# Layer 3's features dealt out through DRAM instead of transposed on TensorE, in a four-layer graph attention kernel

## The chip, the cores and the metric

One core of a Trainium2 chip runs the whole kernel. The metric is the time of one execution on the device in microseconds (us). The engines are TensorE (PE in the profile, its weight loads PEld), VectorE (DVE), ScalarE (ACT), GpSimd (POOL) and SyncE (SP), which here only issues transfers.

## The reference

There are 128 independent graphs of 128 nodes with 512 features, and an adjacency matrix for each. Four layers of graph attention follow each other, each as `x = x + layer(relu(layernorm(x)), adj)`:

```
h  = maximum(layernorm(x), 0)
# layer 0: scores from h @ (W.T a1), h @ (W.T a2); leaky relu, mask, softmax; elu(attn @ h)
# layer 1: xl = h @ W1 (4 heads x 256); attention by head, bias, elu; then a second
#          one-head layer: (elu(..) @ W2), attention over the nodes, bias
# layer 2: scores from h @ w_src, h @ w_dst; softmax; attn @ h
# layer 3: xp = h @ W_proj, split into 8 heads of 64 features
#   scores[h,i,j] = leaky_relu(a_src[h,i] + a_dst[h,j] + b[h]), masked by adj
#   out = relu(softmax(scores) @ xp), heads side by side
```

All is in float32. Layers 1 and 3 project h with a matrix of weights, so TensorE needs h with the features on the partitions; h is made with the nodes on the partitions.

## The kernel before

A graph is one stream of steps, written as a Python generator (`graph`). It runs `layer0` to `layer3` on a tile `xt` of 128 nodes x 512 features, held on chip until the result is written. Up to 13 graphs are in flight (`FLYING`), so that one graph's matmuls fill another's waits. No loop order is written by hand: a planner (`Scheduler`) goes through all streams with a cost for every step and issues, one after the other, the step that can start first. Among steps of the same engine that can start about as early, the older graph goes first, with a due time for each step from a rehearsed graph. The result is one fixed order of instructions on each engine, and each engine works its own list in order. Each wait for data is a semaphore wait in that order.

SyncE's queue carries nearly all transfers. The planner lets 8 of them be under way (`LANES`).

The last five graphs are late (`LATE`): they take other ways, with fewer trips through DRAM, since there is no other graph left to fill the waits.

Steps that matter here:

- `norm_relu` gets mean and variance on VectorE, the factor on GpSimd, and writes h with one ScalarE instruction.
- `transposed` turns up to four 128 x 128 blocks on TensorE into one PSUM bank, and ScalarE copies the bank into a tile. Layers 1 and 3 call it on the four blocks of h, giving `ht`.
- `projected` multiplies `ht`, four blocks as the weights on the array, with `w1x` (three column parts of 344) or `wpx` (two parts of 264). In float32 each block takes two passes: two weight loads and two matmul instructions.
- `rows_in_dram` puts the scores of each head, a column per head, into rows: VectorE transposes 32 x 32 squares, four transfers write the rows to DRAM, and one transfer reads them back to all 128 partitions as `e`.
- `exchanged` moves attention's blocks through DRAM after or before VectorE's 32 x 32 transposes, so TensorE does not transpose them.

A VectorE transpose works on squares of 32 x 32 (`Q` = 32, `R` = 4 squares across the partitions). Its result is a whole transpose only when the squares also trade places, which is what a trip through DRAM can do.

Nearly all instructions are issued from the planner's one line 302, so the profile tells them apart by tile names and shapes: `bank` is a PSUM bank, `ident` the identity that TensorE's transposes use, `h`, `ht`, `wpx`, `w1x` as above, `x` layer 3's projected features (and the second half of layer 1's), `e` the scores, `et` their transposed form, `r` the transposed score columns, `d` the rows in DRAM.

Of the kernel before, what the change touches and what calls it, by code (L numbers as in the profile page):

```python
# [9 lines left out]
F32 = mybir.dt.float32  # L10
I32 = mybir.dt.int32
AF = mybir.ActivationFunctionType
# [314 lines left out]
def kernel(  # L327
# [24 lines left out]
    B, P, D = x.shape  # L352
# [43 lines left out]

    E1, E2, E3 = 2 * H1, 2, 2

    def rows_of(name, n, *shape):
# [19 lines left out]

    def few(to, values):
        with nc.allow_non_contiguous_dma(reason="at most 1024 values, once"):
            nc.scalar.dma_start(out=to, in_=values)

    def setup():
        for i, a in enumerate((l0_a1, l0_a2)):
            few(a0[:, :, i], a.rearrange("(c p) o -> p (c o)", p=P))  # L430
        for i, a in enumerate((l1_src1, l1_dst1)):
            few(a1[:, :, i], a.rearrange("h (c p) -> p (h c)", p=P))
        few(b1, l1_b1.rearrange("(c p) -> p c", p=P))

        w0 = []
        for c in range(KC):
            if c % 2 == 0:
                pair = yield tile_of("e3", 3, H3 * P)
                pair = pair.rearrange("p (c f) -> p c f", c=2)
            w0.append(pair[:, c % 2])  # L440
            yield S.dma_start(out=w0[c], in_=l0_w[c * P : (c + 1) * P])
        yield Fork(fold_u(w0))
        yield from load(0)
        for c in range(KC):
            yield S.dma_start(out=w1x[c][:, E1:], in_=l1_w1[c * P : (c + 1) * P])
        yield Fork(fold_w1())
        yield Fork(load_turned(0))
        yield from load(1)
        yield from load(2)
        vecs = []  # L450
        for row in (l1_src2, l1_dst2):
            vecs.append((yield tile_of("x2", 2, E2 + D))[:, :D])
            yield S.dma_start(out=vecs[-1], in_=row[0].partition_broadcast(P))
        for c in range(FC):
            yield S.dma_start(out=w2x[c][:, E2:], in_=l1_w2[c * P : (c + 1) * P])
        yield Fork(fold_w2(vecs), 3)
        yield S.dma_start(out=b2[:, E2:], in_=l1_b2.partition_broadcast(P))
        yield from load(3)
        yield from load(4)
        for t, row in (w_src, l2_src), (w_dst, l2_dst), (b_l2, l2_b), (b_l3[:, 0], l3_batt):  # L460
            yield S.dma_start(out=t, in_=row.partition_broadcast(P))
        yield from load(5)
        for c in range(KC):
            yield S.dma_start(
                out=wpx[c][:, :, E3:],
                in_=l3_wp[c * P : (c + 1) * P].rearrange("p (h k) -> p h k", h=H3),
            )
        wa = yield tile_of("e3", 3, H3 * P)
        wa = wa[:, : H3 * 2 * K3]
        yield S.dma_start(out=wa, in_=l3_watt.rearrange("h k -> (h k)").partition_broadcast(P))  # L470
        yield Fork(fold_w3(wa), 6)
        for b in range(6, min(FLYING + AHEAD, B)):
            yield from load(b)
# [68 lines left out]
        sched.reached.add("wp")  # L542


    def norm_relu(xt):

        n = nc.vector.BN_STATS_DIM
        st = yield tile_of("st", 6, n + 5)
        yield V.bn_stats(st[:, :n], xt)
        mean, var = st[:, n : n + 1], st[:, n + 1 : n + 2]  # L550
        yield V.bn_aggr(st[:, n : n + 2], st[:, :n])
        ve, rstd, nmr = (st[:, i : i + 1] for i in range(n + 2, n + 5))
        yield G.tensor_scalar(ve, var, EPS, None, ALU.add)
        yield G.tensor_tensor(out=rstd, in0=ve, in1=minus_half, op=ALU.pow)
        yield G.tensor_scalar(nmr, mean, rstd, -1.0, ALU.mult, ALU.mult)
        h = yield tile_of("h", 4, D)
        yield A.activation(out=h, in_=xt, func=AF.Relu, bias=nmr, scale=rstd)
        give_back(st)
        return h

# [44 lines left out]
        yield S.dma_start(out=to, in_=d.rearrange("m b r f -> (m b) (r f)"))  # L605
        return to

    def rows_in_dram(cols, n, heads_inside=False):

        r = yield tile_of("r", 5, Q)  # L610
        yield V.transpose(r, cols)
        d = dram.tile([R, n, Q] if heads_inside else [n, R, Q], F32, tag=f"d{n}", name="d")
        yield Group(
            [
                S.dma_start(
                    out=d[c] if heads_inside else d[:, c], in_=r[c * Q : c * Q + n]
                )
                for c in range(R)
            ]
        )  # L620
        give_back(r)
        return d.rearrange("n c b -> (n c b)").partition_broadcast(P)
# [150 lines left out]

    def layer1(xt, mask, late):
        h = yield from norm_relu(xt)
        ht = yield from transposed(blocks_of(h), "ht", 3)
        give_back(h)
        yield Until("w1")
        fx = yield tile_of("xl", 3, E1 + HF)

        e = yield tile_of("e1", 3, H1 * P)
        if late:
            heads = e.rearrange("p (h c b) -> p h c b", h=H1, b=Q)
        else:
            heads = e.rearrange("p (c h b) -> p h c b", h=H1, b=Q)
        heads = [heads[:, j] for j in range(H1)]

        def rows():
            d = yield from rows_in_dram(fx[:, :Q], H1, not late)
            yield S.dma_start(out=e, in_=d)  # L790

        fork = yield from projected(ht, KC, w1x, 3, columns(fx, 3), rows)
        give_back(ht[0])
        xl = fx[:, E1:]
        yield Join(fork)
        mask = mask.rearrange("p (c b) -> p c b", b=Q)
        c, rz = yield from attention(fx[:, H1:E1], heads, heads, mask)
        for j in range(H1):
            yield A.activation(out=heads[j], in_=heads[j], func=AF.Copy, scale=rz[:, j : j + 1])
        give_back(c)  # L800
        if late:
            et = yield from transposed(blocks_of(e), "et1", 2)
        else:

            yield V.transpose(e, e)
            to = yield from exchanged(e, "et1", 2)
            et = to.rearrange("p (r h b) -> p h r b", h=H1, b=Q)
            et = [et[:, j] for j in range(H1)]
        give_back(e)
        y = yield tile_of("y1", 2, FC, P)  # L810
        for g in range(0, FC, 4):
            po = yield bank()
            yield Group(
                [
                    T.matmul(
                        po[:, (c - g) * P : (c - g + 1) * P],
                        lhsT=xl[:, c * P : (c + 1) * P],
                        rhs=et[c * P // F1],
                        start=True,
                        stop=True,  # L820
                    )
                    for c in range(g, g + 4)
                ]
            )
            yg = y[:, g : g + 4, :]
            yield V.tensor_tensor(
                yg,
                po.rearrange("p (j q) -> p j q", q=P),
                b1[:, g : g + 4].unsqueeze(2).to_broadcast([P, 4, P]),
                ALU.add,  # L830
            )
            give_back(po)

            yg = yg.rearrange("p c q -> p (c q)")
            t = yield tile_of("t", 5, 4 * P)
            yield V.tensor_scalar(t, yg, 0.0, None, ALU.min)
            yield A.activation(out=t, in_=t, func=AF.Exp)
            yield V.scalar_tensor_tensor(yg, t, -1.0, yg, ALU.add, ALU.max)
            give_back(t)
        give_back(fx, et[0])  # L840
        yield Until("w2")
        gx = yield tile_of("x2", 2, E2 + D)

        yl = [y[:, c] for c in range(FC)]
        yield from projected(yl, FC, w2x, 2, columns(gx, 2), plus=columns(b2, 2))
        give_back(y)
        pa, c, rz = yield from attended(gx[:, 1:2], gx[:, 0:1], mask, gx[:, E2:], late)
        give_back(gx)
        yield V.scalar_tensor_tensor(xt, pa, rz, xt, ALU.mult, ALU.add)
        give_back(pa, c)  # L850
# [10 lines left out]
        yield V.scalar_tensor_tensor(xt, pa, rz, xt, ALU.mult, ALU.add)  # L861
        give_back(pa, c)

    def layer3(xt, mask, late):

        h = yield from norm_relu(xt)
        ht = yield from transposed(blocks_of(h), "ht", 3)
        give_back(h)
        yield Until("wp")

        fx = yield tile_of("x3", 3, H3, E3 + K3 + 1)
# [16 lines left out]
            heads = e.rearrange("p (h c b) -> p h c b", h=H3, b=Q)  # L888
        else:
            heads = e.rearrange("p (c h b) -> p h c b", h=H3, b=Q)  # L890
            rows = yield from rows_in_dram(repeated(f[:, 0]), H3, True)
            yield S.dma_start(out=e, in_=rows)
        mask3 = mask.rearrange("p (c b) -> p c b", b=Q)

        for g in range(0, H3, 4):
# [110 lines left out]
    def graph(b):  # L1006
# [23 lines left out]
        yield from layer2(xt, m2, late)  # L1030
        give_back(m2)
        m3 = yield from not_above_0(a, "m3", 3)
        yield from layer3(xt, m3, late)
        yield S.dma_start(out=out[b], in_=xt)

    adjs, adjs_t, xs = {}, {}, {}
# [64 lines left out]
```

## Time and profile before

| | |
|---|---|
| median of 3 runs | 3292.77 us (3290.3 to 3292.96) |
| profiled execution | 3290.5 us |
| its span, first to last instruction | 3288.7 us |
| mean granted TensorE clock | 0.988 |
| TensorE matmul busy | 3233.0 us (98%) |
| VectorE busy | 2839.9 us (86%) |
| ScalarE busy | 2546.5 us (77%) |
| GpSimd busy | 911.3 us (28%) |
| moved by transfers | 412.17 MB in 413584 packets |
| share of the 16 transfer engines, SyncE's queue | 42.9% |

A group's row in the profile reads: line, engine, operation, written tile <- read tiles, shapes, count | busy us in all, mean ns of one | idle time of the engine just before, with what ended it. A timeline row reads: start in us, length in us, engine, line, operation, tiles, shapes, count, and in brackets the idle time before it where there was some. The windows give, for a stretch of time, the busy us and the number of instructions of PE, PEld, DVE, ACT and POOL, then the granted clock, the share of the transfer engines and GB/s. In the slices each digit is a fortieth of the span, in tenths. Ends of matmuls are modelled, so the time between two starts says more than a row's length.

### The profile page before, as it was taken

The numbers are of one execution on the slowest core, as the hardware profiler recorded it, in microseconds if no ns is written. First come the engines' busy times: TensorE is split into PE (matmuls) and PEld (weight loads), VectorE is DVE, ScalarE is ACT, GpSimd is POOL, SyncE is SP. The second block draws the span as 40 slices with busy tenths as digits, with TensorE's granted clock in tenths as the row PEclk, the third lists the DMA queues.
The fourth block names the chain that finished last, engine by engine and source line by source line (L and its number), as shares of the span: only waits on it lengthen the run. The fifth ranks groups of instructions, "written<-read, shape, count | busy, mean of one in ns | idle before, by whom it ended". The sixth has DMA issues, their size and how long they took to land.

```text
span 3288.7 us, 60292 instructions
## 1 busy us (share of the span) xinstructions
PE 3233.0 (98%) x15723; PEld 2529.1 (77%) x15723; DVE 2839.9 (86%) x11308; ACT 2546.5 (77%) x7582; POOL 911.3 (28%) x2313
## 2 busy tenths in 40 slices
PE   6999999999999999999999999999999999999997
PEld 3777777777777777777777777777777777777786
DVE  6778888988888988888898988898888888888875
ACT  3668787887888887777887777887877777877866
POOL 1122223232222232222232322222222222222222
PEclk6999999999999999999999999999999999999998
DMA  6224444444444444444444444444444444444321
GB/s 170 61 82 124 134 129 132 133 127 133 134 126 132 135 126 137 128 128 137 130 132 132 127 132 134 132 133 130 128 134 125 133 137 124 131 136 130 99 89 58
DMA packets 413584, 412.17 MB, mean 125 GB/s; under 512 B 125496, under 2 KB 314040, under 8 KB 413240
## 3 DMA queue, kind: packets, MB, share of 16 engines
q1 hardware_dynamic: 409064, 408.31, 42.9%
q8 instruction: 125, 2.05, 0.3%
q14 instruction: 219, 1.79, 0.2%
q10 hardware_dynamic: 4176, 0.02, 0.1%
HBM read 276.91 MB, written 131.24 MB: 124 GB/s over the span
## 4 chain that ended last, share of the span: by engine, by line
PE 95%; DVE 2%; DMA 2%; ACT 1%; SPq 0%; issue 0%; POOL 0%; ACTq 0%; DVEq 0%; POOLq 0%
PE bank L302 95%; DVE e L302 0%; SPq L302 0%; ACT e L302 0%; DMA d<-r 0%; DVE products L302 0%; DVE t L302 0%; POOL st L302 0%; DMA row<-d 0%; DMA w1x<-in_L_gnn_W_dram 0%; ACT h L302 0%; DMA xt<-in_x_dram 0%; DVE xt L302 0%; DVE st L302 0%; DMA at<-in_adj_dram 0%
## 5 line engine op out<-in xcount | busy, mean ns | idle before, releaser
L302 PE MATMUL bank<-w2x,y 128*128 128x257 f32 x4096 | 959.1, 381 | 0.0
L302 PE MATMUL bank<-w1x,ht 128*128 128x344 f32 x3072 | 954.0, 454 | 1.3 <-ACT ht L302 1.3
L302 PEld LDWEIGHTS bank<-w2x,y 128*128 128x128 f32 x4096 | 768.0, 190 | 171.9 <-issue 51.4
L302 PEld LDWEIGHTS bank<-w1x,ht 128*128 128x128 f32 x3072 | 572.4, 190 | 285.0 <-issue 29.9
L302 ACT ACTIVATE e<-e,f 128x128 f32<-128x128 f32 x2176 | 739.4, 392 | 18.2 <-DVE c L302 18.0
L302 POOL TENSOR_SCALAR st<-st 128x1 f32<-128x1 f32 x1024 | 355.1, 347 | 1041.1 <-DVE st L302 771.8
L302 ACT ACTIVATE e<-e,c 128x128 f32<-128x128 f32 x1408 | 543.5, 396 | 78.7 <-DVE c L302 59.7
L302 PE MATMUL bank<-wpx,ht 128*128 128x264 f32 x2048 | 495.2, 387 | 0.7 <-ACT ht L302 0.7
L302 ACT ACTIVATE h<-xt,st 128x512 f32<-128x512 f32 x512 | 415.1, 812 | 85.6 <-POOL st L302 75.3
L302 PEld LDWEIGHTS bank<-wpx,ht 128*128 128x128 f32 x2048 | 385.0, 191 | 92.1 <-issue 13.6
L302 DVE BATCH_NORM_STATS2 st<-xt 128x6 f32<-128x512 f32 x512 | 349.3, 682 | 0.0
L302 DVE CUSTOM_DVE_ANT_0 e<-e,m 128x128 f32<-128x128 f32 x1496 | 344.0, 284 | 4.2 <-DMA e<-d 3.0
L302 POOL TENSOR_TENSOR st<-st,minus_half 128x1 f32<-128x1 f32 x512 | 313.2, 612 | 40.6 <-POOL st L302 0.2
L302 ACT COPY xl<-bank 128x344 f32<-128x344 f32 x384 | 169.5, 442 | 188.9 <-PE bank L302 187.6
L302 PE MATMUL bank<-h,et 128*128 128x512 f32 x512 | 268.0, 605 | 7.1 <-ACT et L302 7.1
L302 PE MATMUL bank<-et,xl 128*128 128x128 f32 x2048 | 269.5, 275 | 0.0
L302 DVE TENSOR_TENSOR y<-bank,b 128x512 f32<-128x512 f32 x256 | 175.7, 687 | 107.4 <-PE bank L302 106.5
L302 PEld LDWEIGHTS bank<-et,xl 128*128 128x128 f32 x2048 | 254.4, 192 | 13.8 <-issue 1.9
L302 PEld LDWEIGHTS bank<-x,e 128*128 128x128 f32 x1968 | 248.5, 192 | 19.7 <-issue 8.6
L302 POOL TENSOR_SCALAR m<-m 128x128 f32<-128x128 f32 x128 | 86.3, 674 | 619.3 <-DVE m L302 503.8
L302 DVE SCALAR_TENSOR_TENSOR xt<-bank,c,xt 128x512 f32<-128x512 f32 x256 | 192.0, 750 | 75.5 <-PE bank L302 70.3
L302 PE MATMUL bank<-x,e 128*128 128x65 f32 x1968 | 246.7, 268 | 0.0
(83 smaller groups left out, 4475.9 us busy)
## 6 DMA issues: line engine op xcount, KB each, us to landing
e<-d SPq DMA_DIRECT2D x123, 512.0 KB
exchanged<-e SPq DMA_DIRECT2D x492, 128.0 KB
et<-exchanged SPq DMA_DIRECT2D x123, 512.0 KB
xt<-in_x_dram SPq DMA_DIRECT2D x128, 256.0 KB
e<-d SPq DMA_DIRECT2D x128, 256.0 KB
out_dram<-xt SPq DMA_DIRECT2D x128, 256.0 KB
exchanged<-e SPq DMA_DIRECT2D x492, 64.0 KB
et<-exchanged SPq DMA_DIRECT2D x123, 256.0 KB
```

Source lines behind the costliest of these rows:

```text
L302: method(*args, **kw)
```

## The change

For the 123 graphs that are not late, layer 3's h is not transposed on TensorE. ScalarE writes h in another order of columns, VectorE transposes its 32 x 32 squares in place (with a step of four floats between columns), one transfer writes the tile to DRAM, and one reads it back as `ht` in pieces of 512 bytes. In `ht` partition q then holds features 4q to 4q + 3 of each node, next to each other, so a block of weights for TensorE is every fourth float. To match, the rows of layer 3's weights are dealt to the partitions in the same way, four neighbouring rows to a partition.

The late graphs' layer 3 and layer 1 of all graphs still transpose on TensorE, and here too the blocks are every fourth column of h; layer 1's weights are dealt likewise.

Score rows are written by one transfer of 128 x 32 instead of four of 4 x 32 or 8 x 32, and read back in four runs for each partition instead of one. The late graphs' layer 1 keeps the four (`rows_by_head`).

```diff
+    def dealt(w):
+        return w.rearrange("(p c) n -> c p n", c=KC)
...
-            yield S.dma_start(out=w1x[c][:, E1:], in_=l1_w1[c * P : (c + 1) * P])
+            yield S.dma_start(out=w1x[c][:, E1:], in_=dealt(l1_w1)[c])
...
-                in_=l3_wp[c * P : (c + 1) * P].rearrange("p (h k) -> p h k", h=H3),
+                in_=dealt(l3_wp)[c].rearrange("p (h k) -> p h k", h=H3),
...
-    def norm_relu(xt):
+    def norm_relu(xt, dealt=False):
...
-        yield A.activation(out=h, in_=xt, func=AF.Relu, bias=nmr, scale=rstd)
+        to = h
+        if dealt:
+            to = h.rearrange("p (m b k) -> p b m k", b=Q, k=KC)
+            xt = xt.rearrange("p (b m k) -> p b m k", b=Q, k=KC)
+        yield A.activation(out=to, in_=xt, func=AF.Relu, bias=nmr, scale=rstd)
...
+    def features_first(h, plain):
+        if plain:
+            blocks = h.rearrange("p (q k) -> p k q", k=KC)
+            ht = yield from transposed([blocks[:, k] for k in range(KC)], "ht", 3)
+            give_back(h)
+            return ht
+        squares = h.rearrange("p (m b k) -> p m k b", b=Q, k=KC)
+        yield V.transpose(squares, squares)
+        to = yield from dealt_out(h, "ht", 3)
+        give_back(h)
+        blocks = to.rearrange("p (q k) -> p k q", k=KC)
+        return [blocks[:, k] for k in range(KC)]
+
+    def dealt_out(t, tag, bufs):
+        f = t.shape[1] // R
+        d = dram.tile([R, P, f], F32, tag=f"dealt{f}", name="dealt")
+        yield S.dma_start(out=d.rearrange("r (b m) f -> (r b) (m f)", m=R), in_=t)
+        to = yield tile_of(tag, bufs, R * f)
+        yield S.dma_start(
+            out=to.rearrange("p (r f) -> p r f", r=R), in_=d.rearrange("r q f -> q r f")
+        )
+        return to
...
-        d = dram.tile([R, n, Q] if heads_inside else [n, R, Q], F32, tag=f"d{n}", name="d")
+        d = dram.tile([R, Q, Q], F32, tag="squares", name="d")
+        yield S.dma_start(out=d.rearrange("c n b -> (c n) b"), in_=r)
+        give_back(r)
+        rows = d[:, :n].rearrange("c n b -> c (n b)")
+        return rows.unsqueeze(0).to_broadcast([P, R, n * Q])
...
     def layer1(xt, mask, late):
         h = yield from norm_relu(xt)
-        ht = yield from transposed(blocks_of(h), "ht", 3)
-        give_back(h)
+        ht = yield from features_first(h, True)
...
-    def layer3(xt, mask, late):
-        h = yield from norm_relu(xt)
-        ht = yield from transposed(blocks_of(h), "ht", 3)
-        give_back(h)
+    def layer3(xt, mask, late, early):
+        h = yield from norm_relu(xt, not (late or early))
+        ht = yield from features_first(h, late or early)
...
-            rows = yield from rows_in_dram(repeated(f[:, 0]), H3, True)
-            yield S.dma_start(out=e, in_=rows)
+            rows = yield from rows_in_dram(repeated(f[:, 0]), H3)
+            yield S.dma_start(out=e.rearrange("p (c f) -> p c f", c=R), in_=rows)
...
-        yield from layer3(xt, m3, late)
+        yield from layer3(xt, m3, late, b < 0)
```

`early` is never true, since b is at least 0.

More of the change, by code (lines that the diff above doesn't have):

```diff
@@ L606, in exchanged, with rows_in_dram, rows_by_head @@
         return to
-    def rows_in_dram(cols, n, heads_inside=False):
+    def features_first(h, plain):
[19 more added lines that the diff above has]
+        return to
+    def rows_in_dram(cols, n):
         r = yield tile_of("r", 5, Q)
         yield V.transpose(r, cols)
-        d = dram.tile([R, n, Q] if heads_inside else [n, R, Q], F32, tag=f"d{n}", name="d")
-        yield Group(
[L614 to L619, printed above, removed]
+        d = dram.tile([R, Q, Q], F32, tag="squares", name="d")
[3 more added lines that the diff above has]
+        return rows.unsqueeze(0).to_broadcast([P, R, n * Q])
+    def rows_by_head(cols, n):
+        r = yield tile_of("r", 5, Q)
+        yield V.transpose(r, cols)
+        d = dram.tile([n, R, Q], F32, tag="by_head", name="d")
+        yield Group(
+            [S.dma_start(out=d[:, c], in_=r[c * Q : c * Q + n]) for c in range(R)]
         )
@@ L788, in rows @@
         def rows():
-            d = yield from rows_in_dram(fx[:, :Q], H1, not late)
-            yield S.dma_start(out=e, in_=d)
+            if late:
+                d = yield from rows_by_head(fx[:, :Q], H1)
+                yield S.dma_start(out=e, in_=d)
+            else:
+                d = yield from rows_in_dram(fx[:, :Q], H1)
+                yield S.dma_start(out=e.rearrange("p (c f) -> p c f", c=R), in_=d)
         fork = yield from projected(ht, KC, w1x, 3, columns(fx, 3), rows)
```

## Prediction, made before the changed kernel had run

> **What bounds the kernel now.** I read the page first: busy times, the slices with their granted clock, and the chain.
>
> ```profile
> PE 3233.0 (98%) x15723; PEld 2529.1 (77%) x15723; DVE 2839.9 (86%) x11308; ACT 2546.5 (77%) x7582; POOL 911.3 (28%) x2313
> ...
> PE   6999999999999999999999999999999999999997
> ...
> PEclk6999999999999999999999999999999999999998
> ...
> PE 95%; DVE 2%; DMA 2%; ACT 1%; SPq 0%; issue 0%; POOL 0%; ACTq 0%; DVEq 0%; POOLq 0%
> ```
>
> TensorE (PE) is busy from the second slice to the last but one at full clock, and 95% of the chain is its matmuls. Busy matmul time can still hide slack, so next I took the windows over the steady stretch, which give busy us and instruction counts of PE, PEld, DVE, ACT and POOL, then clock and DMA share.
>
> ```profile
> 1000.00:2000.00 1000.00, 1000.00 (x4880) 784.45 (x4879) 891.30 (x3558) 798.12 (x2382) 289.04 (x729) 1.00 0.46 131
> ```
>
> A steady graph has 121 matmul instructions (24 on w1x, 32 on w2x, 16 each on wpx, on xl and on layer 3's e, 6 on attention, 11 transposes), so 4880 are 40.3 graphs at 24.8 us each. Per graph VectorE (DVE) is busy 891.3/40.3 = 22.1 us, ScalarE (ACT) 19.8 us. Then I asked TensorE's timeline for the true pitch, start to start; a row's duration is longer than its pitch, because matmuls overlap.
>
> ```profile
> 1607.43 0.27 PE L302 MATMUL bank<-ident,e 128*128 128x128 f32 x1
> 1607.54 0.60 PE L302 MATMUL bank<-ident,h 128*128 128x128 f32 x4
> 1607.98 1.00 PE L302 MATMUL bank<-x,e 128*128 128x65 f32 x8
> 1608.82 1.08 PE L302 MATMUL bank<-x,et 128*128 128x512 f32 x2
> ...
> 1614.35 1.94 PE L302 MATMUL bank<-wpx,ht 128*128 128x264 f32 x8
> 1616.13 1.90 PE L302 MATMUL bank<-w2x,y 128*128 128x257 f32 x8
> ```
>
> No row has a gap before it. Four feature transposes take 1607.98 - 1607.54 = 0.44 us (0.43 or 0.44 at five other places: mean 0.435), a wpx matmul 1.78/8 = 0.2225, and one of 65 columns 0.84/8 = 0.105. The last is shorter in data than a 128-column weight load, so 0.105 is the pitch of the load itself. The kernel is bound by TensorE's throughput; what leaves TensorE in the steady part leaves the time, if nothing takes its place.
>
> **The change, part by part.** Groups of all instructions with shapes (busy us, mean ns) give the prices of what moves:
>
> ```profile
> L302 ACT ACTIVATE h<-xt,st 128x512 f32<-128x512 f32 x512 | 415.1, 812 | 85.6 <-POOL st L302 75.3 <-issue 3.8 <-PE bank L302 3.0
> L302 ACT COPY ht<-bank 128x512 f32<-128x512 f32 x274 | 157.3, 585 | 49.4 <-PE bank L302 48.5
> L302 DVE STREAM_TRANSPOSE e<-et 128x1024 f32<-128x1024 f32 x123 | 148.6, 1208 | 0.2 <-issue 0.2
> L302 DVE STREAM_TRANSPOSE e<-e 128x512 f32<-128x512 f32 x123 | 86.6, 704 | 4.9 <-ACT e L302 4.9
> L302 POOL TENSOR_TENSOR f<-x,b_l 128x16 f32<-128x16 f32 x128 | 29.7, 232 | 212.5 <-ACT x L302 212.5
> ```
>
> *Removed from TensorE:* the four layer 3 transposes of the 123 graphs that are not late, 492 instructions: 123 x 0.435 = 53.5 us, all on the bounding path. *Removed from ScalarE:* 123 evictions of 0.585, 72 us, off the path. A bank per graph comes free sooner, worth nothing shown.
>
> *Added to VectorE:* 123 transposes of 128x512 in place, their columns four floats apart. The 704 ns row is contiguous; the 1208 ns row has twice the elements and stands for an access at half rate. So 0.70 to 1.21 us a graph, and VectorE goes from 22.1 to between 22.8 and 23.3 of a period of 24.8 - 0.435 = 24.4. TensorE covers it; I take 0.70, the row of equal size. Without that cover the whole 86 to 149 us would show.
>
> *h written in order (block, node, feature):* ScalarE writes runs of four floats. From nothing to a doubled 0.81 us, beside 24.8 - 19.8 = 5 us of ScalarE slack: nothing.
>
> *The trip through DRAM:* 256 KB out, 256 KB back. The longest waits of the chain list show a DRAM leg between 1.53 us (d<-r) and 5.47 us (e<-d), so two legs are 3 to 11 us, less the 0.44 and 0.585 removed. Thirteen graphs are in flight; while the others feed TensorE this costs nothing. It can show where few graphs are in layer 3 yet: up to 11 us once at the start. I take 3, from the nearer, shorter legs, and 2 more (an estimate) for a busier VectorE: 5, range 0 to 13.
>
> *Transfer engines:* they are busy 46% of the steady window. 123 x 512 KB = 63 MB on 408 MB is +15% by bytes; by pieces, 128 rows of 2 KB out, 512 of 512 bytes back, 768 more for the two reads of score rows now in four runs, and some 200 for their writes, about 1600 x 123 = 199,000 on 409,000, or +49%. Between 53% and 69%: not the bound. The far end is possible, as per-piece time is not shown apart; neither end moves my sum.
>
> *SyncE's queue:* four row writes per score set become one, twice a graph; two transfers come. The four took 1.28 to 1.90 us of issue, a single transfer 0.34 to 0.97, so the queue is lighter or even. New waits: the write of dealt waits for VectorE's transpose, the read for the write. In the changed kernel's order, row writes, score reads, et reads and the output stand behind them. Those are waited on by VectorE and TensorE, but VectorE's largest transfer wait now is 50.7 us over the run (row), so the margin is large. Cost taken: none.
>
> *Strided weights:* the disputed part. Rows of w1x and wpx are dealt, so layer 3 loads ht as weights with a step of four floats (16 x 123 loads, plus late graphs), and layer 1 still transposes on TensorE but now loads h with that step (4 x 128). No row has such a load. POOL's f<-x row reads 16 floats 67 apart in 232 ns, no more than its neighbours: the low end, zero. The high end is the load at half clock in the first 40 us, where eight 2-column matmuls go from 27.13 to 28.86: 0.216 each, and four transposes 0.89/4 = 0.22. Under a wpx matmul (0.2225) such a load still hides; a transpose would go from 0.109 to 0.22, 512 x 0.111 = +57 us. I take zero: the trace's only strided read shows none.
>
> [...]
>
> Sum against the profiled execution (3290.5, span 3288.7, 1.8 around it): 3290.5 - 53.5 + 5 = 3242. That execution stands 2.3 us under the median of the runs, 3292.8.
>
> **The rivals.** *A, strided loads cost, and the time goes up.* Place: layer 1's transposes, then the wpx matmuls. Price at the half-rate end: +57 cancels the 53.5, and the exposed first load of 246 wpx groups adds up to 246 x 0.11 = 27: 3290.5 - 53.5 + 57 + 5 + 0 to 27 = 3299 to 3326. It decides from a transpose pitch of about 0.109 + 53.5/512 = 0.214. Past 0.2225 the wpx matmuls stretch too, 16 x 123 = 1968 of them, and each further 0.01 us costs 20 us. For it: no slack in TensorE to hide a longer load at a transpose. Against: only the untested step.
>
> *B, VectorE becomes a bound.* At 23.3 of 24.4 us busy in strict order, short waits add up: if the strided transpose is at its dear end and half to all of the extra 1.21 - 0.70 = 0.51 us reaches the end, 3242 + 123 x (0.255 to 0.51) = 3273 to 3305. For: 89% busy already. Against: TensorE has no gap now.
>
> *C, the longer flight of a graph starves TensorE.* If thirteen graphs only just cover a graph's way, 6 us more per graph stretch the period by 6/13 = 0.46 us: 3290.5 + 123 x (0.46 - 0 to 0.435) = 3294 to 3347. Against: in the steady window TensorE waits for nobody, and ScalarE's largest waits are for TensorE. A planner that places each step by age would show it in gaps before wpx.
>
> That the change doesn't do what it says is hardly open: TensorE's order has 492 fewer transposes.
>
> **How the numbers follow.** The forecast 0.46 (3230 to 3262), A 0.36, B 0.07, C 0.11. Two parts in a thousand, 6.6 us, is about what a measurement of this kernel can tell from no change. All of the forecast is faster; of A 0.05 is faster (a small penalty), 0.08 same, 0.23 slower; of B 0.04, 0.01, 0.02; of C 0, 0.01, 0.10. Together 0.55 faster, 0.10 same, 0.35 slower. The range runs from 3228 (all of 53.5, and 9 us of extra from shorter evictions and a lighter queue) to 3335, which takes in A's half rate and most of C and leaves out loads slower than that. The forecast's own range is 3230 to 3262.
>
> **What would show it.** Right: 532 transposes of h in place of 1024, four of them still 0.43 to 0.44 us apart in layer 1, wpx pitch 0.2225, weight loads still near 190 and 141 ns, TensorE without gaps at 24.4 us a graph, and a VectorE transpose of h at about 0.70. Wrong: transposes of h 0.8 us or more per four with longer load rows (A); TensorE gaps ended by ACT or DVE with VectorE near 97% (B); gaps before wpx ended by the transfer of ht (C).

## The result, and the profile after

The changed kernel takes 3377.83 us (median of 4 runs, 3375.56 to 3382.01) against 3292.86 us for the kernel before in the same series: a ratio of 1.0262, 95% interval 1.0249 to 1.0275. It is 85 us slower where 51 us faster was forecast, and it lies outside the range. The profiled execution spans 3377.8 us at a mean TensorE clock of 0.983.

The busy line and the chain, from the page of the changed kernel:

```profile
PE 3255.4 (96%) x15231; PEld 2607.0 (77%) x15231; DVE 2930.0 (87%) x11431; ACT 2463.3 (73%) x7459; POOL 977.3 (29%) x2313
...
PE 50%; DMA 19%; DVE 19%; ACT 6%; POOL 3%; issue 2%; SPq 1%; ACTq 0%; DVEq 0%
```

TensorE has 492 instructions fewer, as the diff says, and yet 22 us more of busy time. Its share of the chain fell from 95% to 50%: the rest is now transfers and VectorE, in turns. The window over the same steady stretch as before:

```profile
1000.00:2000.00 1000.00, 973.57 (x4580) 783.21 (x4579) 892.94 (x3504) 745.30 (x2269) 304.26 (x704) 1.00 0.54 149
```

A graph now has 117 matmul instructions, so 4580 are 39.1 graphs at 25.5 us; it was 24.8, and 24.4 was forecast. TensorE, without a gap before, idles 26 us of the 1000. The transfer share rose from 0.46 to 0.54, the low end of the forecast. The groups that matter, with shapes:

```profile
L302 PE MATMUL bank<-wpx,ht 128*128 128x264 f32 x2048 | 528.9, 402 | 0.7 <-ACT ht L302 0.7
L302 PEld LDWEIGHTS bank<-wpx,ht 128*128 128x128 f32 x2048 | 500.8, 319 | 15.8 <-ACT ht L302 0.9 <-issue 0.7 <-DVE st L302 0.2
L302 DVE STREAM_TRANSPOSE e<-et 128x1024 f32<-128x1024 f32 x123 | 152.1, 1236 | 77.4 <-DMA et<-exchanged 47.1 <-DMA out_dram<-xt 15.0 <-DMA xt<-in_x_dram 11.0
L302 DVE STREAM_TRANSPOSE h<-h 128x512 f32<-128x512 f32 x123 | 141.5, 1151 | 1.8 <-DMA out_dram<-xt 0.5 <-ACT h L302 0.5
L302 PE MATMUL bank<-x,et 128*128 128x512 f32 x256 | 139.6, 627 | 70.5 <-ACT et L302 70.5
```

Three things differ here from what the prediction took. The wpx weight loads take 319 ns instead of 191. VectorE's transpose of h takes 1151 ns, not the 704 of the contiguous one. And idle time stands where none was: 77.4 us before VectorE's e<-et transposes (0.2 before), ended by transfers, and 70.5 us before TensorE's x,et matmuls (0.6 before). There was 0.7 us of idle time before wpx, as before. The two rows of before for the loads and for x,et:

```profile
L302 PEld LDWEIGHTS bank<-wpx,ht 128*128 128x128 f32 x2048 | 385.0, 191 | 92.1 <-issue 13.6 <-ACT ht L302 1.4 <-DVE f L302 0.5
L302 PE MATMUL bank<-x,et 128*128 128x512 f32 x256 | 133.1, 602 | 0.6 <-ACT et L302 0.6
```

The list of TensorE's waits in the changed kernel, 400 to 3000 us (tile waited for, us in total, times, longest), and TensorE's timeline at one of them:

```profile
PE bank L302 <- ACT et L302: 65.5, 54, 3.0
```

```profile
1526.59 1.06 PE L302 MATMUL bank<-et,xl 128*128 128x128 f32 x8
1529.06 1.12 PE L302 MATMUL bank<-x,et 128*128 128x512 f32 x2 [1.42 <-ACT et L302]
1530.03 1.89 PE L302 MATMUL bank<-w2x,y 128*128 128x257 f32 x8
```

The waiting matmul is the attention of layer 1's second part in one graph; the next, on w2x, is work of another graph, shows no wait of its own and stands behind it in the fixed order. So the stalls are not at the place that was changed. The rows of the other engines just before show how a late transfer gets there:

```profile
1525.43 1.25 DVE L302 STREAM_TRANSPOSE e<-et 128x1024 f32<-128x1024 f32 x1 [1.03 <-DMA et<-exchanged]
1528.08 0.40 ACT L302 ACTIVATE e<-e,c 128x128 f32<-128x128 f32 x1 [2.77 <-DVE e L302]
1528.77 0.24 ACT L302 COPY et<-bank 128x128 f32<-128x128 f32 x1
```

VectorE stands 1.03 us before data that was asked for at 1519.79 us. ScalarE stands 2.77 us behind a later step of VectorE, and only then, in its own order, comes to the copy of et that TensorE waits for.

Long waits cost TensorE time twice here. From 400 to 3000 us its granted clock falls to 0.5 in nine stretches of 3.41 us each, 30.7 us in all, and before the change in none. Each starts within 1.5 us of the end of a wait of 1.8 to 3.0 us; of 15 waits of 1.6 us or more, nine were followed by one. As an estimate, 30.7 us at half clock do 15 us less work. This window lies in the stretch behind the longest wait; the clock stands before the last two numbers:

```profile
1249.00:1252.00 3.00, 3.00 (x13) 2.42 (x13) 2.13 (x6) 1.98 (x5) 0.55 (x1) 0.50 0.94 218
```

The trace's semaphore events give the time from the issue of a transfer to its last landing: medians in us, 400 to 3000 us (90th percentile in brackets where it says more). The last column is the least that the planner counts for it after the change: by its code 0.35 us of issue (0.5 with more than two dimensions), 2.2 of delay, the bytes at 280 KB per us (220 in runs of 512 bytes or less), and 0.3.

| transfer | before | after | new rows in the old order (below) | planned |
|---|---|---|---|---|
| layer 1's score rows e<-d, 256 KB | 3.42 | 5.63 | 5.46 | 4.2 (before: 3.8) |
| layer 3's score rows e<-d, 512 KB | 5.01 | 5.78 | 5.53 | 4.9 (before: 4.7) |
| et<-exchanged, 512 KB | 3.79 (4.55) | 5.95 (8.21) | 4.11 (4.98) | 4.7 |
| et<-exchanged, 256 KB (layer 1) | 2.63 | 2.73 | 2.67 | 3.8 |
| out_dram<-xt, 256 KB | 2.08 (3.81) | 5.37 (6.83) | 2.53 (5.76) | 3.8 |
| xt<-in_x_dram, 256 KB | 2.87 (4.42) | 5.20 (6.41) | 3.27 (6.37) | 3.8 |
| row<-d, 64 KB | 2.97 (3.74) | 3.64 (6.65) | 3.13 (4.10) | 3.2 |
| dealt<-h | none | 3.21 | none | 3.8 |
| ht<-dealt | none | 2.99 | none | 4.2 |

Before, medians lie under the plan but for layer 3's rows. After, the new trip itself and layer 1's et are early, and everything else in the table is late by 0.4 to 1.6 us at the median. Transfers are also asked for late: SyncE issues in a fixed order too, and its waits for VectorE's transposed columns r grew from 203.5 us (132 times) to 506.7 us (250 times) between 400 and 3000 us.

### The profile page after: what moved, and what is told of

It reads as the page before. It is cut to its first block, busy times and chain, and to the rows that moved or that the text cites. A ratio compares the mean times of both kernels' runs of the same rounds, so it can differ in the third digit from the quotient of the medians.

```text
span 3377.8 us, 58573 instructions
## 1 busy us (share of the span) xinstructions
PE 3255.4 (96%) x15231; PEld 2607.0 (77%) x15231; DVE 2930.0 (87%) x11431; ACT 2463.3 (73%) x7459; POOL 977.3 (29%) x2313
## 4 chain that ended last, share of the span: by engine, by line
PE 50%; DMA 19%; DVE 19%; ACT 6%; POOL 3%; issue 2%; SPq 1%; ACTq 0%; DVEq 0%
PE bank L302 50%; DMA out_dram<-xt 4%; DVE e L302 4%; DVE xt L302 4%; DMA et<-exchanged 3%; DMA d<-r 3%; DVE st L302 3%; POOL st L302 3%; DVE t L302 3%; ACT e L302 2%; DMA row<-d 2%; DMA e<-d 2%; DMA dealt<-h 2%; ACT h L302 1%; SPq L302 1%
## 5 line engine op out<-in xcount | busy, mean ns | idle before, releaser
L302 PE MATMUL bank<-w2x,y 128*128 128x257 f32 x4096 | 970.1, 382 | 0.0
L302 ACT ACTIVATE e<-e,c 128x128 f32<-128x128 f32 x1408 | 525.6, 395 | 285.3 <-DVE e L302 179.3
L302 PE MATMUL bank<-wpx,ht 128*128 128x264 f32 x2048 | 528.9, 402 | 0.7 <-ACT ht L302 0.7
L302 PEld LDWEIGHTS bank<-wpx,ht 128*128 128x128 f32 x2048 | 500.8, 319 | 15.8 <-ACT ht L302 0.9
L302 POOL TENSOR_TENSOR st<-st,minus_half 128x1 f32<-128x1 f32 x512 | 366.2, 715 | 39.2 <-POOL st L302 0.2
L302 DVE STREAM_TRANSPOSE e<-et 128x1024 f32<-128x1024 f32 x123 | 152.1, 1236 | 77.4 <-DMA et<-exchanged 47.1
L302 PE MATMUL bank<-x,et 128*128 128x512 f32 x256 | 139.6, 627 | 70.5 <-ACT et L302 70.5
```

The costliest lines, as they stand in the source:

```text
L302: method(*args, **kw)
```

## The experiments

The theories: *trips* (transfers land later than the fixed order was planned for, so TensorE waits in it), *step* (the step of four floats costs on TensorE or VectorE), *flight* (thirteen graphs no longer suffice), and *rows* (the new score rows, by their transfers or by their place in the order).

### The score rows alone

Layer 3's trip and the dealing are undone; only the score rows are new.

```diff
-        return w.rearrange("(p c) n -> c p n", c=KC)
+        return w.rearrange("(c p) n -> c p n", c=KC)
...
-            blocks = h.rearrange("p (q k) -> p k q", k=KC)
-            ht = yield from transposed([blocks[:, k] for k in range(KC)], "ht", 3)
+            ht = yield from transposed(blocks_of(h), "ht", 3)
...
-        yield from layer3(xt, m3, late, b < 0)
+        yield from layer3(xt, m3, late, True)
```

> Only the score rows' change: one write of 128x32 instead of four, read back in four runs; layer 3 and layer 1 transpose on TensorE from contiguous blocks as before, weights not dealt. Theory S (strided access is what costs: VectorE's transpose at 1.15 us and weight loads at 319 ns, and the strict order behind them passes it on): as before, 3286 to 3298. Theory D (the added transfers and pieces make every trip through DRAM later, and that starves TensorE): part of it is here, 768 pieces more per graph, so 3300 to 3330. Theory P (the planner's new order is simply worse): open, 3285 to 3330.

Measured: 3325.68 us, ratio 1.0102 (1.0087 to 1.0117). TensorE is busy 993.45 of the steady 1000 us. So 33 us of loss come with the part that the prediction put at nothing.

### The rows in the old order, and the old rows in the new one

Three kernels separate instructions from order. In the first, the new rows' transfers are planned at the old costs, which leaves the order on the compute engines exactly that of the kernel before. In the second, the old rows are planned at the new costs. The third keeps the old order and the four old writes, and takes only the read in four runs.

```diff
+    def as_if(self, busy, moves, lanes=1):
+        self.busy, self.moves, self.lanes = busy, moves, lanes
+        return self
...
-        yield S.dma_start(out=d.rearrange("c n b -> (c n) b"), in_=r)
+        yield S.dma_start(out=d.rearrange("c n b -> (c n) b"), in_=r).as_if(
+            4 * 0.35, 4 * (n * Q * 4 / 130e3), 4
+        )
```

> The instructions of the kernel with score rows alone (one write of 128x32, read in four runs), but the planner is given the old steps' costs and lanes, so the order on TensorE, VectorE and ScalarE is that of the kernel before. Theory P (the planner's other order makes the loss of 33 us, not the transfers themselves): 3285 to 3297, with TensorE's idle time in the steady window below 1 us in 1000. Theory D (the row transfers themselves are slower, in more pieces): 3315 to 3330.

> The instructions of the kernel before (four row writes, one run for each read), but the planner is given the costs and lanes of the new row steps, so the order on TensorE, VectorE and ScalarE is that of the kernel with score rows alone. Theory P: it takes the loss with it, 3318 to 3345 (four writes where one was planned make SyncE's queue later still). Theory D: 3285 to 3300.

> As the run with new rows in the old order (3320), but the rows are written by four transfers as before; only the read in four runs per partition is new. The order on the compute engines is that of the kernel before. If the read's pieces cost (four of 512 or 1024 bytes instead of one of 2048 or 4096): 3312 to 3325. If the single write of 128 pieces costs: 3288 to 3300.

Measured: new rows in the old order 3319.98 us, 1.0087 (1.0072 to 1.0102); old rows in the new order 3295.41 us, 1.001 (1.0 to 1.002); four writes with the read in runs 3346.90 us, 1.0168 (1.0153 to 1.0183). The order is innocent. The read in runs costs 54 us, and the single write gives 27 of them back. In the first of the three (400 to 3000 us), VectorE does not wait for the slow read itself (e<-d: 2.9 us, 3.0 before). It waits for row<-d, the row of the other attentions, more than twice the 43.9 us of before:

```profile
DVE e L308 <- DMA row<-d: 95.1, 60, 4.3
```

SyncE's queue shows a way from the one to the other. Once for every four graphs it issues four transfers of the next adjacency (at_t). With the read in runs this takes 4.98 us at the median instead of 3.01, and the small write d<-r that row<-d needs is issued only then. The same place in the order, before and with the new rows:

```profile
1397.12 2.47 SPq L302 DMA_DIRECT2D at_t<-in_adj_dram  x4
1399.69 0.50 SPq L302 DMA_DIRECT2D d<-r  x1
```

```profile
1420.14 5.61 SPq L308 DMA_DIRECT2D at_t<-in_adj_dram  x4
1425.84 0.83 SPq L308 DMA_DIRECT2D d<-r  x1
```

The chain of work runs from the second of these writes over row<-d to ScalarE's et, and TensorE's x,et matmul there starts after a wait of 1.38 us. That these places make up all of the 28 us is not shown.

### The new rows in layer 3 only, in the old order

Layer 1 writes and reads its rows as before.

```diff
-                d = yield from rows_in_dram(fx[:, :Q], H1)
-                yield S.dma_start(out=e.rearrange("p (c f) -> p c f", c=R), in_=d)
+                d = yield from rows_inside(fx[:, :Q], H1)
+                yield S.dma_start(out=e, in_=d)
```

> The kernel before, with the new score rows in layer 3 alone (one write, read in four runs of 1024 bytes); layer 1's rows as before; the order on the compute engines is that of the kernel before. If layer 1's read in pieces of 512 bytes is what costs (it landed in 5.46 us instead of 3.42, layer 3's in 5.53 instead of 5.01): 3288 to 3300. If both reads cost by their bytes: 3305 to 3320.

Measured: 3292.95 us, 0.9997 (0.9988 to 1.0007). Layer 3's new rows are free, and the four transfers of the adjacency are issued in 3.11 us again. The whole 28 us are layer 1's, which are read to all 128 partitions in runs of 512 bytes instead of one of 2048. Layer 3's runs are 1024 bytes.

### The kernel before with an unused trip

Each graph that is not late also sends xt out and reads it back into a spare tile, 256 KB each way, in the pieces of the change; the planner counts nothing for it.

```diff
+        yield S.dma_start(
+            out=d.rearrange("r (b m) f -> (r b) (m f)", m=R), in_=xt
+        ).unplanned(5.0)
+        yield S.dma_start(
+            out=spare.rearrange("p (r f) -> p r f", r=R), in_=d.rearrange("r q f -> q r f")
+        ).unplanned(0.0)
```

> The kernel before, with the trip of h through DRAM added and used by nobody: per graph 256 KB written from xt and read back in pieces of 512 bytes into a spare tile, planned at no cost, so that the order on the compute engines is exactly that of the kernel before. The result is the reference's. Theory D (transfers, their queue or the eight lanes are loaded so far that two more of them per graph make all others late): 3310 to 3350, with more idle time before the reads of row and e. Theory P alone (only the changed order and its thin margins cost): 3289 to 3297.

Measured: 3298.91 us, 1.0022 (1.0012 to 1.0032). The load of the trip costs 6 us. Its queue line on the page shows 49.8% against 42.9%, so the share alone is not what hurts:

```profile
q1 hardware_dynamic: 491720, 472.81, 49.8%
```

### The step of four floats

First on the kernel with the new rows only: all transposes on TensorE, loading every fourth column of h, and the weights dealt. The order on every compute engine stays the same.

```diff
-            ht = yield from transposed(blocks_of(h), "ht", 3)
+            blocks = h.rearrange("p (q k) -> p k q", k=KC)
+            ht = yield from transposed([blocks[:, k] for k in range(KC)], "ht", 3)
```

> The score rows' change and the dealt weights; all of layer 3 and layer 1 transpose on TensorE, from every fourth column of h; no trip of h through DRAM, no VectorE transpose of h; layer 3's loads of ht are contiguous again. Theory S: only 1024 transposes' loads are strided, four in 0.47 us instead of 0.44, so 3293 + 256 x 0.035 = 3302 (3296 to 3310). Theory D: as the kernel with score rows alone, 3300 to 3330. If loads at a step of four floats were the whole of the loss, this would be some 30 us above the kernel with score rows alone.

Measured: 3334.56 us, 1.0127 (1.0112 to 1.0143), 9 us over the rows alone. The loads of h take 207 ns against 142, and start to start they are 0.119 us apart against 0.109: 1024 x 0.010 = 10 us.

Second, the whole change with steps of two floats in place of four ("pairs"): ht is read in 1024 pieces of 256 bytes, and layer 1's columns are contiguous.

```diff
-            to = h.rearrange("p (m b k) -> p b m k", b=Q, k=KC)
+            to = h.rearrange("p (m b k) -> p b m k", b=Q, k=2)
...
-        blocks = to.rearrange("p (q k) -> p k q", k=KC)
-        return [blocks[:, k] for k in range(KC)]
+        blocks = to.rearrange("p (a n k) -> p a k n", a=2, k=2)
+        return [blocks[:, a, k] for a in range(2) for k in range(2)]
```

> All of the change except the step of four: h's squares and ht in pairs of features, so VectorE's transpose and layer 3's weight loads have a step of two floats; the read of ht comes in 1024 pieces of 256 bytes instead of 512 of 512; layer 1 as before. Theory S: VectorE's transpose 0.70 us, wpx loads 190 ns, TensorE without gaps: 3235 to 3250. Theory D: the trips are as long or longer, so 3370 to 3400 whatever the transposes cost. If a step of two costs as much as one of four, it stays near 3378 and tells nothing between them.

Measured: 3379.44 us, 1.0261 (1.0226 to 1.0295). Its groups:

```profile
L302 PEld LDWEIGHTS bank<-wpx,ht 128*128 128x128 f32 x2048 | 401.3, 198 | 64.1 <-ACT ht L302 1.1 <-issue 0.9 <-PE bank L302 0.6
L302 DVE STREAM_TRANSPOSE h<-h 128x512 f32<-128x512 f32 x123 | 86.5, 703 | 1.8 <-ACT h L302 1.0
```

The order on every compute engine is that of the changed kernel. Every price of the step is gone, and the time has not moved: TensorE's waits for et grew from 65.5 to 86.8 us instead, and its time at half clock from 30.7 to 54.6 us. As long as late transfers pace the kernel, cheaper matmuls only wait longer.

### The planner told of the transpose, and fourteen graphs

```diff
+            if name == "transpose" and len(outs[0].shape) == 4:
+                return 1.07, 0.12
```

> The changed kernel with one number of the planner changed: VectorE's transpose of h is planned at 1.07 us instead of 0.60, the same instructions in another order. Theory S in the form that the plan's error does the harm: most of the loss is regained, 3270 to 3320, TensorE's idle time in the steady window below 10 us in 1000. Theory S in the form that VectorE and TensorE simply lack the time: 3350 to 3390. Theory D: unchanged, 3370 to 3390.

Measured: 3410.48 us, 1.0357 (1.0331 to 1.0383). Correcting the plan's error on VectorE's transpose does not help; in this order TensorE waits more, not less, 74.3 us against 65.8 from 400 to 3000 us. It also shows that another order of the same instructions can by itself move the time by 33 us. Then pairs with one more graph in flight:

```diff
-FLYING = 13
+FLYING = 14
```

> The kernel with pairs (all of the change, no step of four) with 14 graphs in flight instead of 13, nothing else. Theory C (thirteen graphs do not cover a graph's longer flight): the period falls to 13/14 until TensorE binds, so 3240 to 3290. Theory P: another order of the same kind, 3350 to 3400, up or down. Theory D, with the transfer engines or the queue as the bound: 3370 to 3390.

Measured: 3474.36 us, 1.0563 (1.0544 to 1.0582). More graphs in flight make it worse: TensorE waits 130.2 us for et, VectorE 146.1 for e<-d. *Flight* in its plain form falls. Why the fourteenth graph costs so much stays open.

### Longer trips in the plan

One line changes: the delay that the planner adds to a transfer (large, small).

```diff
-            return busy, (2.2 if moved > 16384 else 1.3)
+            return busy, (3.7 if moved > 16384 else 2.3)
```

On pairs, on the change itself, and on the kernel before:

> The kernel with pairs with two numbers of the planner changed: a large transfer lands 3.7 us after its issue in its plan instead of 2.2, a small one 2.3 instead of 1.3; the same instructions in another order. If the loss is that the plan takes the trips through DRAM for shorter than they are, so that engines stand before late data in a strict order (theory P in its precise form): most of the gain comes back, 3250 to 3310. If transfers or engines lack the time: 3370 to 3400.

> The changed kernel with the two numbers of the planner changed (a large transfer lands after 3.7 us in its plan instead of 2.2, a small one after 2.3 instead of 1.3), the same instructions. The same edit took the kernel with pairs from 3379 to 3325. If the step of four floats costs beside that: 3325 + 16 x 123 x 0.0115 + 512 x 0.009 = 3352 from TensorE alone, up to 3385 with VectorE's 0.45 us. If it costs nothing even with the stalls gone: 3320 to 3335.

> The kernel before with the same two numbers of the planner changed, as a control. If longer planned trips help wherever the plan is too tight and harm nothing else: 3285 to 3300. If the four row writes per set then fill the eight lanes in the plan (they take four lanes each), the plan itself has gaps on TensorE and the time rises: 3330 to 3420.

Measured: pairs 3325.19 us, 1.0104 (1.0089 to 1.0119), 54 us regained; the change itself 3341.60 us, 1.0148 (1.0132 to 1.0163), 36 regained; the kernel before 3452.0 us, 1.0489 (1.0473 to 1.0504). The wait for et shrinks from 86.8 us to

```profile
PE bank L302 <- ACT et L302: 26.4, 33, 1.0
```

in pairs. That fits *trips*: no transfer was changed, only the order was given more room. But the landings moved with the order: in pairs the 512 KB et<-exchanged went from 6.04 to 5.02 us, out_dram<-xt from 5.49 to 3.40 and xt<-in_x_dram from 5.31 to 4.04. And TensorE's 54.6 us at half clock are gone. How much of the 54 us is room, how much earlier landings and how much the clock is not shown. The control shows that more room is not good everywhere. A likely reason, argued only: in the kernel before four row writes hold four of the planner's eight places for longer. And the step of four now costs 16 us (3341.60 - 3325.19).

### Layer 1's rows as before, step and trips one after the other

All three have the change with layer 1's rows undone (the edit shown above) and their own plan: with the step of four, with pairs, and with pairs and trips of 3.2 and 2.0 us.

> The changed kernel with one part undone: layer 1's score rows are written by four transfers and read in one run, as before. The planner makes its own order for it. If that read is a large part of the loss: 3310 to 3350. If the planner's too short trips alone decide: 3360 to 3390.

> As the run before it, and with pairs, so without a step of four floats: the same plan, so the difference is what strided access costs there. From TensorE and VectorE's times: 10 to 40 us less than the run before it. If stalls hide it, as with the changed kernel and pairs: within 5 us of it.

> As the run before it, with the planner told of longer trips (3.2 us instead of 2.2 for large transfers, 2.0 instead of 1.3 for small ones). If layer 1's read and the short plan were all of the loss, the forecast gain appears: 3240 to 3275, with TensorE idle under 5 us in 1000. If more is wrong: 3290 to 3330.

Measured: 3386.98 us, 1.0281 (1.0265 to 1.0296); 3365.42 us, 1.0221 (1.0197 to 1.0244); 3287.62 us, 0.998 (0.9971 to 0.9989). Undoing the slow read alone regains nothing, though most landings are good again: in the first kernel the 512 KB et<-exchanged lands in 4.29 us, out_dram<-xt in 2.52, xt<-in_x_dram in 3.98, and transfers hold 3% of the chain instead of 19%. In this order TensorE waits for another step, 46.0 us for layer 1's ht and 15.1 for et, and is at half clock for 54.6 us. At one such wait for ht, of 1.96 us before 1529.74 us, the chain holds ScalarE's steps one after the other and no transfer. So late data is not what this order mostly waits for. With the longer trips the waits are 22.5 and 8.5 us, the longest 1.5, and there is no half clock: the third kernel is the first to beat the one before, by 5 us. The first two have the same order, and the step of four costs 22 us there. The last step was then turned back to four:

> After, with layer 1's score rows as before and trips planned at 3.2 and 2.0 us. Against the run of the same with steps of two floats (3287.6 us) only the step of four differs; TensorE's order of instructions is the same in both. If the step of four costs the sum of its longer rows on TensorE, wpx groups of eight stretch from 8 x 0.2225 to 8 x 0.234 (123 x 16 x 0.0115 = 23 us), h loads cost 512 x 0.035 x a part (up to 18 us), so 3305 to 3328 us. If VectorE's 1.15 us against 0.70 adds to it: up to 55 us more, 3340 to 3380. If the step is hidden: 3285 to 3292.

Measured: 3321.06 us, 1.0085 (1.007 to 1.01). This is the cleanest pair of all: TensorE's order is the same, instruction by instruction, and so are its waits. Steady windows with steps of two, then four:

```profile
1000.00:2000.00 1000.00, 986.31 (x4716) 773.00 (x4715) 900.88 (x3594) 769.93 (x2334) 294.26 (x726) 1.00 0.56 153
```

```profile
1000.00:2000.00 1000.00, 986.30 (x4662) 791.97 (x4662) 905.29 (x3563) 759.09 (x2306) 290.19 (x716) 1.00 0.55 151
```

TensorE is equally busy and does 54 matmuls less. TensorE's timeline shows where, steps of two first: a group of eight wpx matmuls takes 1.78 us to the next start, then 1.87.

```profile
1252.96 1.94 PE L302 MATMUL bank<-wpx,ht 128*128 128x264 f32 x8
1254.74 1.90 PE L302 MATMUL bank<-w2x,y 128*128 128x257 f32 x8
```

```profile
1240.67 2.03 PE L302 MATMUL bank<-wpx,ht 128*128 128x264 f32 x8
1242.54 1.90 PE L302 MATMUL bank<-w2x,y 128*128 128x257 f32 x8
```

Over 400 to 3000 us the mean start-to-start time goes from 0.2227 to 0.2363 us for wpx and from 0.1528 to 0.1637 for transposes of h, waits included: 1968 x 0.0136 + 512 x 0.0109 = 32 us, and 33 were measured. VectorE is busy 2918.8 against 2874.9 us, and nothing is left for that to have cost.

### The planner told of ScalarE's h

In the 3287.62 us kernel TensorE's remaining waits (400 to 3000 us) are 22.5 us for layer 1's ht and 8.5 for et. The ht comes from a ScalarE write of h that takes 0.81 us and is planned at 0.655. So: trips of 2.7 and 1.6, and

```diff
-            busy = n * 0.00081 + 0.105 + (0, 0.075, 0.135)[pointers]
+            busy = n * 0.00081 + 0.105 + (0, 0.075, 0.29)[pointers]
```

> Steps of two floats, layer 1's rows as before, trips planned at 2.7 and 1.6 us, and the planner told that ScalarE's write of h takes 0.81 us instead of 0.655. In the 3287.6 us run TensorE's remaining waits, 22.5 us of 31 in 400 to 3000 us, are for layer 1's ht behind ScalarE's h: if the plan's error on that step makes them, and trips at 2.7 and 1.6 are long enough, they go and the time is 3255 to 3275. If the shorter planned trips bring the late transfers back: 3300 to 3340, with TensorE's waits for et again. If telling a planner the truth about one step only shuffles the order: 3285 to 3300.

Measured: 3273.53 us (3268.05 to 3277.65), ratio 0.9941 (0.9924 to 0.9957), the fastest of all. Its steady window, and TensorE's two waits from 400 to 3000 us:

```profile
1000.00:2000.00 1000.00, 999.03 (x4794) 783.86 (x4793) 901.80 (x3654) 781.09 (x2371) 310.45 (x735) 1.00 0.57 155
```

```profile
PE bank L302 <- ACT et L302: 3.3, 6, 1.1
PE bank L302 <- ACT ht L302: 3.3, 9, 0.6
```

4794/117 = 41.0 graphs, 24.4 us each: the forecast's period, with transfers at 0.57, higher than in the change as it was made. Two things were changed at once here, so how much each brought is not shown.

## Why the prediction was wrong, step by step

**Bound and removal: right.** TensorE bounds the kernel, and taking out 492 transposes is worth what was said, 24.8 to 24.4 us a graph, once nothing else holds it back.

**"While the others feed TensorE this costs nothing": the step that failed most.** It took the thirteen graphs in flight as cover for any delay. But the order is fixed, so a matmul whose data is late holds all that stand behind it, however many other graphs are ready. The cover is the room that the planner left for each transfer, 4.7 us for the et that VectorE waits for and that now lands in 5.95. A planner counts on its own numbers; the prediction looked at TensorE's gaps before, found none, and did not ask how much later a transfer could land before one appears. Planning longer trips was worth 54 us in pairs and 3386.98 - 3321.06 = 66 us with layer 1's rows undone; the second of these came in an order in which TensorE mostly waited for ScalarE's ht, so it is the fixed order's price, but not a late transfer's alone. Nor did the prediction price the half clock behind long waits, as an estimate 15 us in the changed kernel and 27 in pairs (half of 30.7 and 54.6).

**"Cost taken: none" for the score rows.** The prediction weighed the read in four runs as pieces on the transfer engines, and SyncE's issue time. It did not price a read that lands later and what stands behind it in the queue. Layer 1's read went from 3.42 to 5.46 us in the old order, and that cost 28 us there, with the gain of the single write already in it. The wait for row, so small that the prediction called the margin large (43.9 us from 400 to 3000 us), became 95.1.

**"I take zero: the trace's only strided read shows none" for the weights.** The row chosen, 16 floats on GpSimd, was too far away. The loads take 319 ns, 1.67 times 191. Rival A's clause, wpx stretching past the pitch that hides a load at 20 us for each 0.01, is what happened: 0.0136, 27 us. Its other price was too high, since transposes of h went to 0.12 us and not 0.22. Of A's 84 us at most, 33 came.

**"I take 0.70" for VectorE's transpose.** It took 1.15, near the dear end. The cover by TensorE held: that error cost nothing that the runs can show, so rival B falls.

**Rival C** named the right symptom, TensorE starved by longer flights, at the wrong place (gaps before wpx) and by the wrong limit (the number of graphs). The gaps came before layer 1's attention.

**The rest:** the unchanged write of h, 0.812 us, was right, and the load of the trip was 6 us.

The sum, made again from the runs: forecast 3242; 31 over it in the best version; 14 more without its two changes of the plan; 33 for the step of four; 66 that the longer planned trips had given back; 9 less with layer 1's new rows, in again another order: 3242 + 31 + 14 + 33 + 66 - 9 = 3377. Each term is the step from one measured kernel to the next, so the sum must come out and proves nothing by that. The parts hide each other, so another order of undoing gives other sizes: the rows alone cost 33, and the step cost 0, 16, 22 or 33. The 33 for the step is measured in one order; the 66 is the effect of an edit whose shares (late data, ScalarE's waits, the clock) stay open. The rivals were set against one another, while A's price and C's symptom came together.

Of the 31 us some lie at the ends. In the first 600 us the best version's TensorE is busy 552.1 us against 562.8 before. After that it issues 12744 matmuls in 2670.4 us, which at the steady 4.794 per us would be 2658.3. What causes these was not tried.

## What to carry to other kernels

In a pipeline whose order is fixed ahead, other work in flight does not by itself cover a late transfer; the room planned between its issue and its use has to: here 4.7 us were planned for the 512 KB et, and it landed in 5.95. So before adding transfers to such a kernel, compare the landing times in the trace with those the plan counts on, for the transfers already there as well as for the new ones, and look in the granted clock behind long waits, which here stood at 0.5 for 3.41 us behind nine waits of 1.8 to 3.0 us. And an edit that shows no effect while something else holds the pace (pairs, layer 1's rows) is not thereby free or harmless: try it again once that is mended.

## What the runs showed of the hardware

A step of two floats cost nothing to speak of here and a step of four much, on two engines: TensorE's weight loads of ht took 191 ns contiguous, 197 with two and 319 with four; VectorE's 128x512 transpose 704, 703 and 1151. Why four floats apart is slower stays open.

The longer load did not simply stretch the matmul: with 121 ns more per load (318 against 197) the wpx pitch rose by 14 ns (0.2227 to 0.2363 us), so most of it still ran beside other matmuls.

A read of the same DRAM rows to all 128 partitions landed later with shorter runs: 256 KB in 512 pieces of 512 bytes took 5.46 us, the same bytes in runs of 2048 bytes 3.42. The read of ht has as many pieces of the same size, from different addresses, and landed in 2.99 us in the changed kernel. Why the shared one is slower stays open.

TensorE's granted clock fell to 0.5 behind long waits: in the changed kernel, from 400 to 3000 us, for 3.41 us at a time behind nine of 15 waits of 1.6 us or more. In the first kernel with layer 1's rows undone all 16 stretches at half clock, 54.6 us in all, came at the end of waits of 1.66 us or more; the 3287.62 us kernel, whose longest wait is 1.5 us, has none from 400 to 3000 us.
